# Graph layers on one Trainium2 core: the second message layer's attribute map computed with the first layer's, and smaller first pieces of the next layer's input

## The chip, the cores and the metric

The kernel runs on one core of a Trainium2 chip. The metric is the device time of one execution in microseconds (us); for the kernel before it is the median of three runs. A core has a matrix engine (TensorE, PE in the profile, with its weight loads as PEld), a vector engine (VectorE, DVE), an engine for functions of one element (ScalarE, ACT), GpSimd (POOL) and a queue engine (SyncE, SP). Matmuls read SBUF and write PSUM; DVE and ACT read both.

## The reference

A graph has N = 6250 nodes with 64 features and E = 200,000 edges, each with 16 attributes. First come two SAGE layers (mean over the incoming neighbours, a linear map, 64 to 128 to 64), a residual and a layer norm. Then come three message layers, which the change is about:

```python
def _mp_layer(x, src_f, dst_f, ea_f, W, b):
    m = concatenate([x[dst_f], x[src_f], ea_f], axis=1) @ W.T + b
    return relu(segment_sum(m, dst_f, num_segments=n))
h = _mp_layer(x, ..., W0, b0); h = relu(_batchnorm(h, g0, be0))
h = _mp_layer(h, ..., W1, b1); h = relu(_batchnorm(h, g1, be1))
h = _mp_layer(h, ..., W2, b2)
```

The edges include a self loop for each node with attributes of one. The result is a layer norm of x + h. Since the map is linear, a layer's sum over a node's edges falls into three parts: count times the node's own mapped features; the sum of the mapped features of its sources; and a part of the attributes alone, W's last 16 columns times the node's sum of attributes, and the bias times its count. The third part depends on no features, only on the layer's weights.

## The kernel before, in words

Nodes lie in NB = 49 blocks of P = 128; 4 blocks make a tile of TW = 512, of which there are NT = 13 (the last with one block). The kernel first builds the adjacency as dense fp8 counts, tile by tile (`build`), stores it in DRAM (`adj8`), and runs the first SAGE layer along with it. The second SAGE layer also builds the sums of attributes (`attributes`, L1008): `ext`, a tile of 128 partitions and 6272 nodes. Its rows 0 to 47 are the attribute sums three times (high, middle and low parts in bf16), rows 48 to 63 are zero, and rows 64 to 127 hold the node's count with the self loop. The weights for it are `extT[n]` (L577): three copies of the layer's attribute columns in rows 0 to 47 and the bias in row 64 = D (L603).

A sum over neighbours is `aggregate` (L640). For each block of destinations it adds 49 matmuls (`product`, L650): an adjacency block 128x128 as weights, and the source block's features as three bf16 parts side by side (192 columns) as the moving operand. With `terms`, one more float32 matmul per block, `term` (L657), adds the attribute part: 128 nodes of `ext` as weights and 64 columns of `extT[n]` moving, and it shows as two records. In layers two and three (n = 1, 2) `terms` is set (L1167). `add_parts` (L674) then adds the three parts on DVE.

Tiles 0 and 1 of a layer are done together and source by source (`src_first`), since their products can start as soon as the first sources are known; `feed` (L1171) makes the sources ready. In these two tiles the order before was: all eight terms, then for each source block `feed` and its eight products. `feed` calls `next_input` (L1108) for pieces of four blocks, one piece ahead: ACT makes `y` from the former layer's `hr` (a fused batch norm and ReLU, L1112), PE multiplies each block with `maps[n - 1]` into `u` (L1115), ACT and DVE split it into three bf16 parts (`split`, L626) and DVE makes the node's own part `own` (L1118, L1119). The matmuls of a program are reordered by a scheduler unless `pin` holds one behind the instruction that was written ahead of it on its engine.

At the end of a tile, layer one (`first_message`, L1125) transposes on PE (L700), copies on ACT (L702, `mx`), and multiplies with `catT[0]` (L1136) and `extT[0]` (L1137) into `lin`, of which ACT makes `hr` with a ReLU (L1138); layer two (`message_layer`, L1141) adds `own` (L1147), transposes into `tr` (L1151) and applies the ReLU on ACT (L1152). DVE takes the batch statistics of `hr` (L1123). Behind the last tile come `bn_aggr` (L1193), the square root on ACT (L1195) and four small DVE steps (L1196 to L1199) that give scale and shift `sc`. Only then can `next_input` of the following layer start. The adjacency tiles are loaded into three buffers, on SP's and ACT's queues in turn (`load_adj`, L677).

Of the kernel before, what the change touches and what calls it, by code (L numbers as in the profile page):

```python
# [11 lines left out]
F32 = mybir.dt.float32  # L12
# [462 lines left out]
def gnn_kernel(ctx: ExitStack, tc: tile.TileContext, x, src, dst, ea, W_l1, b_l1, W_r1, W_l2, b_l2, W_r2,  # L475
# [71 lines left out]
    with ExitStack() as fast:  # L547
# [22 lines left out]
        for n in range(3):  # L570


            if n == 0:
                catT.append(const.tile([2 * D, D], F32, name="catT"))
            else:
                maps.append(const.tile([D, 2 * D], F32, name=f"maps{n}"))
            extT.append(const.tile([P, D], F32, name=f"extT{n}"))  # L577
            nc.vector.memset(extT[n], 0.0)

        def load_weights():  # L580
            def transposed(to, of, at=0):
                p = psm.tile([P, P], F32, name="tr")
                k, m = of.shape
                pin(nc.tensor.transpose(p[:m, :k], of, ident[:k, :k]))
                nc.scalar.copy(to, p[:m, :k])

            def load(to, of):
                load.turn = not load.turn
                pin((nc.sync if load.turn else nc.scalar).dma_start(to, of))

            load.turn = False
            load(bl1, b_l1.rearrange("(p o) -> p o", o=1))
            load(bl2, b_l2.rearrange("(o d) -> o d", o=1).to_broadcast([P, D]))
            for to, w in ((w1s[:D, :], W_l1), (w1s[D:, :], W_r1), (w2s[:, :D], W_l2), (w2s[:, D:], W_r2)):
                t = spare(w.shape[1])[: w.shape[0], :]
                load(t, w)
                transposed(to, t)
            for n, (w, b) in enumerate(((W0, b0), (W1, b1), (W2, b2))):
                t = spare(2 * D + 3 * EC)[:D, :]
                for r in range(3):  # L600
                    load(t[:, 2 * D + r * EC: 2 * D + (r + 1) * EC], w[:, 2 * D:])
                load(t[:, : 2 * D], w[:, : 2 * D])
                load(extT[n][D: D + 1, :], b.rearrange("(o d) -> o d", o=1))  # L603
                if n == 0:
                    transposed(catT[0], t[:, : 2 * D])
                else:
                    transposed(maps[n - 1][:, D:], t[:, : D])
                    transposed(maps[n - 1][:, : D], t[:, D: 2 * D])
                transposed(extT[n][: 3 * EC, :], t[:, 2 * D:])
            for n, (g, be) in enumerate(((g0, be0), (g1, be1))):  # L610
                gam.append(const.tile([D, 1], F32, name=f"gam{n}"))
                bet.append(const.tile([D, 1], F32, name=f"bet{n}"))
                load(gam[n], g.rearrange("(p o) -> p o", o=1))
                load(bet[n], be.rearrange("(p o) -> p o", o=1))
# [25 lines left out]
        def aggregate(psa, pt, tiles, n, src_first=False, feed=None, terms=None, sources=range(NB)):  # L640

            views = [view(a, j) for a, j in tiles]
            sums = [psa.tile([P, 4, TW // 2], F32, name="agg") for _ in tiles]
            blocks = [(k, i) for k, (_, j) in enumerate(tiles) for i in range(tw(j) // P)]

            def product(k, i, b):

                nc.tensor.matmul(sums[k][:, i, :n], views[k][:, b, i * P: (i + 1) * P], pt[:, b, :n],  # L650
                                 start=(b == sources[0] and terms is None and not (src_first and i % 2)), stop=(b == sources[-1]),
                                 skip_group_check=src_first or terms is not None)

            def term(k, i):
                if terms is not None:
                    at = tiles[k][1] * TW + i * P
                    nc.tensor.matmul(sums[k][:, i, : terms[1].shape[1]], terms[0][:, at: at + P], terms[1],  # L657
                                     start=not (src_first and i % 2), stop=False, skip_group_check=True)

            if src_first:  # L660
                for k, i in blocks:
                    term(k, i)
                for b in sources:
                    feed(b)
                    for k, i in blocks:
                        product(k, i, b)
            else:
                for k, i in blocks:
                    term(k, i)
                    for b in range(NB):  # L670
                        product(k, i, b)
            return sums
# [61 lines left out]
        with ExitStack() as bld:  # L734
# [319 lines left out]
            hot = bld.enter_context(tc.tile_pool(name="ahot", bufs=2))  # L1054
            lhss = [ew.tile([P, EAG, P], BF16, name=f"lhs{k}", bufs=1) for k in range(2)]
            for lhs in lhss:
                nc.gpsimd.memset(lhs[:, :, 3 * EC: D], 0.0)
                nc.gpsimd.memset(lhs[:, :, D:], 1.0)
            selfl = ew.tile([P, 1], F32, name="selfl", bufs=1)
            nc.vector.memset(selfl, 0.0)  # L1060
            nc.vector.memset(selfl[:EC, :], 1.0)
            nc.vector.memset(selfl[D:, :], 1.0)


            per = -(-NSUB // NT)
# [33 lines left out]

        mp = fast.enter_context(tc.tile_pool(name="fmp", bufs=1))  # L1100
        hr = mp.tile([D, NPAD], F32, name="hr")
        own = mp.tile([P, NB, D], F32, name="own")
        ok_s = mp.tile([1, 1], I32, name="ok_s")
        psu = fast.enter_context(tc.tile_pool(name="fpsu", bufs=2, space=PSUM))
        nc.sync.dma_start(ok_s, ok_d)
        nc.vector.tensor_single_scalar(inv, cnt, 1.0, ALU.add)

        def next_input(n, b, sc, pt):  # L1108

            nb, s = min(4, NB - b), slice(b * P, min(b + 4, NB) * P)  # L1110
            y = work.tile([D, TW], F32, name="h1")
            nc.scalar.activation(y[:, : nb * P], hr[:, s], AF.Relu, bias=sc[:, 1:2], scale=sc[:, 0:1])  # L1112
            u = psu.tile([P, 4, P], F32, name="u")
            for i in range(nb):
                nc.tensor.matmul(u[:, i, :], y[:, i * P: (i + 1) * P], maps[n - 1], start=True, stop=True)  # L1115
            split(pt[:, b: b + nb, : 3 * D], u[:, :nb, :D], nb)
            o = own[:, b: b + nb, :]
            nc.vector.tensor_mul(o, u[:, :nb, D:], inv[:, b: b + nb].unsqueeze(2).to_broadcast([P, nb, D]))  # L1118
            nc.vector.tensor_add(o, o, u[:, :nb, :D])  # L1119
# [5 lines left out]
        def first_message(j, ps, stats):  # L1125

            w, s = tw(j), slice(j * TW, j * TW + tw(j))
            nb, bs = w // P, j * TW // P
            h = res[:, bs: bs + nb, :]
            nd = work.tile([P, 4, P], F32, name="nd")  # L1130
            nc.gpsimd.tensor_tensor(nd[:, :nb, :D], h, inv[:, bs: bs + nb].unsqueeze(2).to_broadcast([P, nb, D]), ALU.mult)  # L1131
            add_parts(nd[:, :nb, D:], ps, nb)
            nc.vector.tensor_add(nd[:, :nb, D:], nd[:, :nb, D:], h)
            both = transposed_tile(nd, nb)
            pm = psm.tile([P, TW], F32, name="lin")
            nc.tensor.matmul(pm[:D, :w], catT[0], both[:, :w], start=True, stop=False)  # L1136
            nc.tensor.matmul(pm[:D, :w], extT[0], ext[:, s], start=False, stop=True)  # L1137
            nc.scalar.activation(hr[:, s], pm[:D, :w], AF.Relu)  # L1138
            statistics(j, stats)

        def message_layer(n, j, ps, stats):  # L1141
# [6 lines left out]
            if n < 2:  # L1148
                t = psm.tile([P, 4, P], F32, name="tr")
                for i in range(nb):  # L1150
                    nc.tensor.transpose(t[:D, i, :], v[:, i, :], ident)  # L1151
                nc.scalar.activation(hr[:, s], t[:D, :nb, :].rearrange("f i p -> f (i p)"), AF.Relu)  # L1152
                statistics(j, stats)
                return
            nc.vector.scalar_tensor_tensor(v[:, :nb, :], v[:, :nb, :], 0.0, res[:, bs: bs + nb, :], ALU.max, ALU.add)
# [8 lines left out]
        sc = None  # L1164
        for n in range(3):
            pt = parts[n % 2]
            terms = (ext, extT[n]) if n else None  # L1167
            stats = work.tile([D, NT, nc.vector.BN_STATS_DIM], F32, name="stats") if n < 2 else None
            first = [(load_adj(j), j) for j in range(2)]

            def feed(b):  # L1171
                if n and b % 4 == 0:
                    if b == 0:
                        next_input(n, 0, sc, pt)
                    if b + 4 < NB:
                        next_input(n, b + 4, sc, pt)

            def message(j, ps):
                if n == 0:
# [11 lines left out]
                break  # L1191
            mv = work.tile([D, nc.vector.BN_AGGR_DIM], F32, name="mv")
            nc.vector.bn_aggr(mv, stats.rearrange("p j s -> p (j s)"))  # L1193
            sc = work.tile([D, 2], F32, name="sc")
            nc.scalar.activation(sc[:, 0:1], mv[:, 1:2], AF.Sqrt, bias=eps_t[:D])  # L1195
            nc.vector.reciprocal(sc[:, 0:1], sc[:, 0:1])  # L1196
            nc.vector.tensor_mul(sc[:, 0:1], sc[:, 0:1], gam[n])
            nc.vector.tensor_mul(sc[:, 1:2], mv[:, 0:1], sc[:, 0:1])
            nc.vector.tensor_sub(sc[:, 1:2], bet[n], sc[:, 1:2])  # L1199
        ok_r = nc.values_load(ok_s[0:1, 0:1], min_val=0, max_val=1)  # L1200

    with tc.If(ok_r == 0):
# [32 lines left out]
```

## Time and profile before

| | us |
|---|---|
| median of 3 runs (1628.0 to 1630.6) | 1628.94 |
| the profiled execution | 1625.03 |
| its span, first to last instruction | 1623.2 |
| PE busy in it | 1496.0 |
| DVE busy | 908.1 |
| ACT busy | 571.7 |
| products L650, 12,005 records | 1090.6 busy |

The span begins with the building of the adjacency; the three message layers start at about 919 us. The change from layer one to layer two lies at 1136 to 1151 us, the one from two to three at 1379 to 1390 us. Matmuls are pipelined, so the lengths of their records overlap, and the time that one takes is read from the starts. "Granted clock" is the share of its full clock that TensorE had in a stretch.

### The profile page before, as it was taken

Reading aid. Unit: us, or ns where it says so; the run is one execution under the profiler, and the core shown is the slowest. Engines: PE = TensorE matmul, PEld = TensorE weight load, DVE = VectorE, ACT = ScalarE, POOL = GpSimd, SP = SyncE. Lnnn points to the kernel's source line nnn. Section 1 sums busy time; section 2 is a strip of 40 time slices with the busy share of each in tenths; the row PEclk is TensorE's granted clock in tenths of the full one; section 3 lists DMA queues with packets and bytes.
Section 4 is the critical chain, followed back from the end, with each engine's and each line's share of the span. In section 5 each row is a group of like instructions: output and inputs, shape, how many; then the busy total and the mean of one; then the engine's idle time right before and its main releaser. Section 6 shows DMA issues by size and latency. Waiting matters only on the chain.

```text
span 1623.2 us, 38529 instructions
## 1 busy us (share of the span) xinstructions
PE 1496.0 (92%) x17135; PEld 1381.1 (85%) x17135; DVE 908.1 (56%) x1536; ACT 571.7 (35%) x1067; POOL 206.5 (13%) x94
## 2 busy tenths in 40 slices
PE   3687899999998999999999999999999999999997
PEld 1475787888887898999899988888899999899997
DVE  4999999997987618987986511111431111442222
ACT  2717475777866514444654200000310000310000
POOL 2344752441601100000000000000000000000000
PEclk9586899999999999999999999999899999899999
DMA  5121332140420645535344354443245443255440
GB/s 137 50 80 36 115 103 89 82 165 9 166 84 1 276 174 201 203 130 205 133 141 138 145 239 160 159 173 122 125 169 216 174 160 147 112 222 193 176 179 11
DMA packets 44432, 227.31 MB, mean 140 GB/s; under 512 B 23622, under 2 KB 30851, under 8 KB 36544
## 3 DMA queue, kind: packets, MB, share of 16 engines
q1 hardware_dynamic: 36571, 139.22, 22.8%
q10 hardware_dynamic: 4932, 78.28, 12.3%
q0 software_dynamic: 2752, 7.26, 1.5%
q8 instruction: 136, 2.23, 0.6%
q14 instruction: 41, 0.33, 0.1%
HBM read 183.77 MB, written 42.57 MB: 139 GB/s over the span
## 4 chain that ended last, share of the span: by engine, by line
PE 64%; DVE 19%; ACT 7%; issue 4%; DMA 4%; SPq 0%; ACTq 0%; POOL 0%; DVEq 0%
PE agg L650 48%; PE pair L962 7%; DVE lo L620 7%; ACT a L969 4%; DVE rhs L620 3%; PE u L1115 2%; PE bank L1029 2%; DVE e L1020 1%; DMA a<-adj 1%; DVE e L1022 1%; PE agg L657 1%; DMA e<-in_edge_attr_dram 1%; DVE nd L675 1%; DMA parts<-in_L_gnn_W_dram 1%; PE lin L1136 1%
## 5 line engine op out<-in xcount | busy, mean ns | idle before, releaser
L650 PE MATMUL agg<-parts,a 128*128 128x192 bf16 (+1 forms) x12005 | 1090.6, 246 | 3.1 <-DVE nd L675 1.7
L650 PEld LDWEIGHTS <-a 128*128 128x128 fp8e3 x12005 | 1007.4, 98 | 20.7 <-issue 11.8
L969 ACT ACTIVATE a<-pair 128x784 fp8e3<-128x784 f32 (+3 forms) x355 | 292.1, 894 | 113.8 <-PE pair L962 112.2
L962 PE MATMUL pair<-rhs,lo 128*128 128x147 bf16 (+5 forms) x2569 | 267.6, 245 | 53.1 <-DVE lo L620 19.0
L962 PEld LDWEIGHTS <-lo 128*128 128x128 bf16 x2569 | 198.8, 104 | 106.2 <-issue 49.0
L620 DVE TENSOR_TENSOR rhs<-iota,k 128x1960 bf16<-128x1960 f16 (+15 forms) x240 | 238.6, 1015 | 12.4 <-PE pair L962 10.4
L620 DVE TENSOR_TENSOR lo<-iota,k 128x2048 bf16<-128x2048 f16 x161 | 195.0, 1214 | 0.3 <-PE pair L962 0.3
L675 DVE TENSOR_REDUCE z<-agg 128x256 f32<-128x768 f32 (+1 forms) x39 | 35.3, 910 | 282.2 <-PE agg L650 281.9
L858 POOL DMA_INDIRECT rows<-ends,start_i x42 | 143.7, 3420 | 202.2 <-DVE key L870 157.1
L620 DVE TENSOR_TENSOR lo<-iota,e_d 128x2048 bf16<-128x2048 f16 (+11 forms) x132 | 130.8, 1011 | 20.5 <-PE bank L1029 18.3
L1029 PE MATMUL bank<-lo,lhs 128*128 128x128 bf16 x1701 | 107.5, 219 | 16.7 <-ACT lhs L1023 11.4
L1029 PEld LDWEIGHTS <-lhs 128*128 128x128 bf16 x1701 | 98.3, 98 | 28.2 <-ACT lhs L1023 19.5
L675 DVE TENSOR_REDUCE nd<-agg 128x256 f32<-128x768 f32 (+1 forms) x26 | 23.4, 905 | 116.0 <-PE agg L650 116.0
L1131 POOL TENSOR_TENSOR nd<-res,inv 128x256 f32<-128x256 f32 (+1 forms) x13 | 7.6, 588 | 549.1 <-DVE z L1078 339.2
L1123 DVE BATCH_NORM_STATS2 stats<-hr 64x6 f32<-64x512 f32 (+1 forms) x26 | 17.0, 652 | 101.7 <-ACT hr L1138 80.4
L702 ACT COPY mx<-tr 128x512 f32<-128x512 f32 (+1 forms) x26 | 14.7, 565 | 161.9 <-PE tr L700 161.9
L691 ACT ACTIVATE sp_r<-z 128x256 f32<-128x256 f32 (+1 forms) x26 | 10.5, 403 | 172.8 <-DVE z L690 172.8
L1152 ACT ACTIVATE hr<-tr 64x512 f32<-64x512 f32 (+1 forms) x13 | 7.3, 565 | 179.9 <-PE tr L1151 179.9
L1019 ACT CAST lhs<-e 128x512 bf16<-128x512 f32 (+21 forms) x72 | 36.1, 502 | 62.8 <-PE bank L1029 44.2
L821 POOL DMA_INDIRECT parts<-in_dst_dram,pos x22 | 41.7, 1897 | 50.8 <-DVE pos L816 38.3
L1020 DVE TENSOR_TENSOR e<-e,lhs 128x512 f32<-128x512 f32 (+21 forms) x72 | 39.4, 551 | 12.9 <-ACT lhs L1019 12.7
L1021 ACT CAST lhs<-e 128x512 bf16<-128x512 f32 (+21 forms) x72 | 36.3, 505 | 23.4 <-DVE e L1020 21.9
(131 smaller groups left out, 805.8 us busy)
## 6 DMA issues: line engine op xcount, KB each, us to landing
a<-adj SPq DMA_DIRECT2D x24, 3136.0 KB, 10.8
a<-adj ACTq DMA_DIRECT2D x24, 3136.0 KB, 11.5
adj<-a SPq DMA_DIRECT2D x12, 3136.0 KB, 10.7
e<-in_edge_attr_dram SPq DMA_DIRECT2D x25, 256.0 KB, 2.6
a<-adj SPq DMA_DIRECT2D x4, 784.0 KB
out_dram<-z SPq DMA_DIRECT2D x12, 128.0 KB, 6.4
e<-in_edge_attr_dram SPq DMA_DIRECT2D x7, 152.0 KB, 2.2
adj<-a SPq DMA_DIRECT2D x1, 784.0 KB
```

What stands on the lines that cost most here:

```text
L620: nc.vector.tensor_tensor(to.rearrange("p g (h two) -> p g h two", two=2), iota[:, :n].rearrange("p (h two) -> p h two", two=2).unsqueeze( ...
L650: nc.tensor.matmul(sums[k][:, i, :n], views[k][:, b, i * P: (i + 1) * P], pt[:, b, :n], start=(b == sources[0] and terms is None and not ( ...
L675: nc.vector.tensor_reduce(to, ps[:, :nb, : 3 * D].rearrange("p b (r d) -> p b d r", r=3), AX.X, ALU.add)
L821: pin(nc.gpsimd.indirect_dma_start(out=blks[t % most], out_offset=None, in_=dst.rearrange("(e o) -> e o", o=1), in_offset=bass.IndirectOff ...
L858: pin(nc.gpsimd.indirect_dma_start(out=rows[:, i, :], out_offset=None, in_=end[:, :], in_offset=bass.IndirectOffsetOnAxis(ap=start_i[:, t: ...
L962: nc.tensor.matmul(pair[:, bank % 2, col: col + wc], lo_hot(t, c), rhs[:, i, :wc], start=first, stop=last)
L969: nc.scalar.activation(av[:, :, o: o + 2 * nd].rearrange("p h (two d) -> p h two d", two=2), pair[:, :, : nd * NB].rearrange("p two (d h) ...
L1019: nc.scalar.copy(lhs[:, :g, 0:EC], r)
L1020: nc.vector.tensor_sub(r, r, lhs[:, :g, 0:EC])
L1021: nc.scalar.copy(lhs[:, :g, EC:2 * EC], r)
L1029: nc.tensor.matmul(ps[:, :P], lhs[:, q, :], oh[:, q % HOT, :], start=(c == 0 and q == 0), stop=(i == last_b[b] and q == g - 1))
L1115: nc.tensor.matmul(u[:, i, :], y[:, i * P: (i + 1) * P], maps[n - 1], start=True, stop=True)
```

## The change

The maps of layers one and two stand side by side in one tile `ext01` (128x128). In layer one the matmul with `ext` now gives 128 output rows: 64 for layer one and 64 for layer two's attribute part. DVE takes the latter out of PSUM, clamped to finite values, and puts it into rows 64 to 127 of `ext` (`e1`), which layer one has read by then. The bias moves to row 48, and the count's rows are 48 to 127, so the rows that stay (48 to 63) are enough. Layer two has no terms; instead DVE adds `e1` to the transposed sums ahead of the ReLU. Layer three keeps its terms, with `ext`'s 128 rows (the rows of `extT[2]` from 64 on are zero).

The order at the start of a layer changes: the first piece has one block, the second three, the others four; the matmuls `u` and the terms are pinned; the terms stand behind the first `feed`. In the scale's chain the mean is negated on its own and the last two DVE steps become one.

```diff
-            extT.append(const.tile([P, D], F32, name=f"extT{n}"))
+            if n == 0:
+                ext01 = const.tile([P, 2 * D], F32, name="ext01")
+            extT.append(ext01[:, n * D: (n + 1) * D] if n < 2 else const.tile([P, D], F32, name="extT2"))
...
-                load(extT[n][D: D + 1, :], b.rearrange("(o d) -> o d", o=1))
+                load(extT[n][3 * EC: 3 * EC + 1, :], b.rearrange("(o d) -> o d", o=1))
...
+                    if src_first:
+                        pin(first)
             if src_first:
-                for k, i in blocks:
-                    term(k, i)
                 for b in sources:
                     feed(b)
+                    if b == sources[0]:
+                        for k, i in blocks:
+                            term(k, i)
...
-                nc.gpsimd.memset(lhs[:, :, 3 * EC: D], 0.0)
-                nc.gpsimd.memset(lhs[:, :, D:], 1.0)
+                nc.gpsimd.memset(lhs[:, :, 3 * EC:], 1.0)
...
+        e1 = ext[D:, :]
...
-        def next_input(n, b, sc, pt):
+        def next_input(n, b, end, sc, pt):
...
-                nc.tensor.matmul(u[:, i, :], y[:, i * P: (i + 1) * P], maps[n - 1], start=True, stop=True)
+                pin(nc.tensor.matmul(u[:, i, :], y[:, i * P: (i + 1) * P], maps[n - 1], start=True, stop=True))
...
-            nc.tensor.matmul(pm[:D, :w], catT[0], both[:, :w], start=True, stop=False)
-            nc.tensor.matmul(pm[:D, :w], extT[0], ext[:, s], start=False, stop=True)
+            nc.tensor.matmul(pm[:, :w], ext01, ext[:, s], start=True, stop=False, skip_group_check=True)
+            nc.tensor.matmul(pm[:D, :w], catT[0], both[:, :w], start=False, stop=True, skip_group_check=True)
             nc.scalar.activation(hr[:, s], pm[:D, :w], AF.Relu)
+            nc.vector.tensor_scalar(e1[:, s], pm[D:, :w], 3e38, -3e38, ALU.min, ALU.max)
...
-                nc.scalar.activation(hr[:, s], t[:D, :nb, :].rearrange("f i p -> f (i p)"), AF.Relu)
+                nc.vector.tensor_add(hr[:, s], t[:D, :nb, :].rearrange("f i p -> f (i p)"), e1[:, s])
+                nc.scalar.activation(hr[:, s], hr[:, s], AF.Relu)
...
-            terms = (ext, extT[n]) if n else None
+            terms = (ext, extT[n]) if n == 2 else None
...
-                if n and b % 4 == 0:
-                    if b == 0:
-                        next_input(n, 0, sc, pt)
-                    if b + 4 < NB:
-                        next_input(n, b + 4, sc, pt)
+                ends = [1] + list(range(4, NB, 4)) + [NB]
+                if n and b == 0:
+                    next_input(n, 0, ends[0], sc, pt)
+                if n and b in [0] + ends[:-1]:
+                    q = ([0] + ends).index(b)
+                    if q + 1 < len(ends):
+                        next_input(n, ends[q], ends[q + 1], sc, pt)
...
+            nc.vector.tensor_single_scalar(mv[:, 0:1], mv[:, 0:1], -1.0, ALU.mult)
...
-            nc.vector.tensor_mul(sc[:, 1:2], mv[:, 0:1], sc[:, 0:1])
-            nc.vector.tensor_sub(sc[:, 1:2], bet[n], sc[:, 1:2])
+            nc.vector.scalar_tensor_tensor(sc[:, 1:2], sc[:, 0:1], mv[:, 0:1], bet[n], ALU.mult, ALU.add)
```

## The prediction

> **What bounds the kernel now.** I read the page first, then TensorE's timeline inside the message layers, then the chain of waits around the two layer changes, then the granted clock in stretches.
>
> ```profile
> span 1623.2 us, 38529 instructions
> PE 1496.0 (92%) x17135; PEld 1381.1 (85%) x17135; DVE 908.1 (56%) x1536; ACT 571.7 (35%) x1067; POOL 206.5 (13%) x94
> PEclk9586899999999999999999999999899999899999
> PE 64%; DVE 19%; ACT 7%; issue 4%; DMA 4%; SPq 0%; ACTq 0%; POOL 0%; DVEq 0%
> ```
>
> The change works behind 936 us, in the three message layers. TensorE (PE) carries the chain there: between 1195.0 and 1378.8 us it is busy 182.2 of 183.8 us, VectorE (DVE) 23.9, ScalarE (ACT) 7.1. What leaves PE in such a stretch leaves the time; what lands on DVE or ACT there is free. One block of the second layer (start, length, what):
>
> ```profile
> 1206.67 0.36 PE L657 MATMUL agg<-extT,ext 128*128 128x64 f32 x2
> 1206.87 4.21 PE L650 MATMUL agg<-parts,a 128*128 128x192 bf16 x49
> 1210.91 0.36 PE L657 MATMUL agg<-extT,ext 128*128 128x64 f32 x2
> ```
>
> The two records of a term (L657) start 0.20 us ahead of the products, and 49 products fill the other 4.04 us: lengths overlap, so I count starts. The chain at the change from layer one to two, and from two to three:
>
> ```profile
> 1136.67 1.76 PE agg L657 x16
> 1138.43 1.00 PE lin L1136 x2
> ...
> 1141.12 0.43 PE lin L1136 x2
> ...
> 1143.65 0.16 DVE sc L1198
> ...
> 1144.02 0.82 ACT h L1112
> 1144.84 0.04 issue
> 1144.89 3.79 PE u L1115 x16
> ```
> ```profile
> 1378.98 1.76 PE agg L657 x16
> 1380.74 0.12 PE tr L1151
> ```
>
> Both times eight terms of the next layer run ahead of the last matmuls of the old one, PE then idles 3.11 and 3.18 us while mean, variance and scale are formed and ACT makes a 512-column input (0.82 us). And the clock (stretch, busy PE and count, granted clock, DMA share, GB/s):
>
> ```profile
> 496.21:499.62 3.41, 1.41 (x11) 1.00 0.00 0
> 1141.33:1144.74 3.41, 0.44 (x4) 1.00 1.04 449
> 1144.74:1148.15 3.41, 3.26 (x15) 0.50 0.89 383
> 1148.15:1151.56 3.41, 3.32 (x17) 0.50 0.02 7
> 1151.56:1154.97 3.41, 3.41 (x23) 0.50 0.00 0
> 1154.98:1158.39 3.41, 3.41 (x41) 1.00 0.02 5
> ```
>
> In this trace the clock changes only on a grid of 3.41 us. A stretch with a thin PE is followed by half clock, and it comes back only behind a stretch full of products: the two full of 64-row `u` matmuls did not bring it back. At 1383.67 to 1393.91 it is the same: 10.2 us at half clock, some 5.1 us lost, at each layer change.
>
> **Terms of layer two, tiles 2 to 12.** 10 tiles of four blocks and one of one: 41 terms x 0.20 = 8.2 us off a full PE. Nothing is late in their place: a tile then takes 16.2 us, and the matrix loads land 10 to 13 us behind their issue with three buffers. In return each tile of layer one gets a DVE pass 64x512 out of PSUM (`e1`), and each of layer two an addition 64x512 ahead of the ReLU. Nearest row: 128x256 out of PSUM 0.42 us, so some 0.7 us each by columns. DVE has 160 us free there; inside the layers both cost nothing.
>
> **The wider attribute map, layer one.** Same two passes of 512 columns (0.59 us a record) with 128 output rows for 64; weight loads 0.19 for 0.14 us, beside running matmuls. The term now comes ahead of `catT`, which still waits for `mx`. 0, between -0.3 and +0.6 us over 13 tiles.
>
> **First layer change.** The eight terms go: `lin` of tile 11 starts at 1136.51 instead of 1138.36, 1.85 us, and the transpose of tile 12 behind it needs nothing later (its `nd` is ready at 1137.4). The scale chain loses one DVE step, 0.19 us (the negation runs under ACT's square root; if it holds that up, 0). The first input is one block: the nearest rows for 64x128 on ACT are 0.27 (the ReLU of tile 12) and 0.49 us (the last input); I take 0.3, near the ReLU, saving 0.5. `e1` of tile 12 (some 0.28 us) runs beside ACT's ReLU, which reads the other 64 partitions of the same bank. Here a rule speaks against the change: the Trainium skill, "PSUM — Partial Sum Buffer", section "PSUM bank collisions raise a hardware error", forbids two engines in one bank and one 32-partition quadrant at a time. The quadrants differ here, so no wait is owed; were one put in by bank, it would cost 0.3 to 0.9 us. No row of before shows it; I take 0. Sum: 2.55 us.
>
> **Second layer change.** Without terms ahead of it the transpose of tile 12 starts when its input is ready (1379.64) and not at 1380.58: 0.83. Scale chain 0.19, short input 0.5, less 0.3 for the added DVE step (128 columns 0.22 and a hop): 1.2 us gained. The terms are now pinned behind the first two `u` pieces: 16 records x 0.12 = 1.9 us of full-clock work that formerly lay partly in idle time. Behind them on PE are queued all products of the layer.
>
> **Pieces of one and three blocks, pinned.** `u` needs as many matmuls as before (98), but now one piece ahead instead of three. From the end of a `u` piece its split takes 2.3 us (1150.83 to 1153.11); behind it PE has 32 products and the next `u`, 2.75 + 1.08 = 3.8 us, so no stall. At the start `u` of blocks 1 to 3 covers the split of block 0 roughly: 0.1 us. The second adjacency tile, issued at 1131.73, lands at 1144.5, about when the first product would be ready: 0, up to 1 us.
>
> **The clock.** The rule: the Trainium skill, "TensorE: Matmul & The Clock Gate", Part 1, says half rate comes after an idle window of some 3.4 us and full rate after one busy window. By it the new gaps (3.11 - 0.7 = 2.4 us; 3.18 - 0.4 = 2.8 us) would keep full rate: another 5 us off at each change, sum 22. The trace decides otherwise: both old gaps are under 3.4 us and dropped, and at 496 us a stretch still 1.41 us busy dropped; return took three windows. I let both drop. When does the clock return? First change: the first long run of products is 24 x 0.165 = 4.0 us between `u` pieces, beginning 5.5 us in; a window fits it or the next run, 8 to 14 us in, against 10: 0, with 2 us either way. Second change: terms and the first products are 5.2 us of 128-row matmuls from 2.2 us on; a window fits by 4.6 to 8 us, mean 6.3 against 9.9: half of 3.6 us, 1.8 us gained. That counts the float32 terms as activity; if they don't, -2 instead. The second change: 1.2 - 1.9 + 1.8 = 1.1 us.
>
> **Rest.** Two memsets of ones instead of four on POOL, one more small one on DVE, a bias row at 48: 0, within 0.5.
>
> **Sum.** 8.2 + 2.55 + 1.1 = 11.9 us. The profiled execution took 1625.03 us (span 1623.2 and 1.8 around it) and would take 1613.1. The three timed runs have their median 3.9 us above it; I keep that: 1628.94 - 11.9 = 1617.0 us.
>
> **Rivals.**
> - As summed, 70%: 1613.5 to 1620.5 by the bounds above.
> - The clock survives a layer change, 12%: 5 us more for one (1612), 10 for both (1607). For: shorter gaps, and a grid line in mid-gap halves each side. Against: the drop at 496 us.
> - The layers start badly, 9%: `u` pieces between the first products keep a window from filling, so the half clock lasts one or two windows longer at each change (1.7 us each), or the second tile's load is awaited: 1620.5 to 1624.
> - The terms leave, but PE waits for something else (loads, sums' buffers), 4%: only the first layer change pays, 1626. Against: three buffers and 1.6 us of idle PE in 184 us.
> - Slower, 5%: the pinned order, one piece ahead. If split and own sums of a piece, sharing DVE and ACT with the next input, take longer than 3.8 us from `u`, every one of some 24 pieces stalls by the excess. It eats the 11.9 us from a split of 4.3 us on; at 5 us it costs 29 us, 1646. Against: 2.3 us in the trace.
>
> **How the numbers follow.** Likeliest 1617.0. Range 1609.5 to 1622.5: the first case, the clock surviving once, the milder half of the bad starts; about 15% is left out. About 0.2%, 3.3 us, is what a measurement can tell from no change. Faster 0.91, within 0.04 (lost gain), slower 0.05.
>
> **What would show it.** Records of L657 fall from 196 to 98, and the second layer's block from 4.24 to 4.04 us; if blocks stay at 4.24, the main step is wrong. PE's gaps at the layer changes shrink to about 2.4 and 2.8 us. Half clock is seen behind both, the second shorter than 10.2 us; a clock at 1.00 there is the second case. Idle PE ahead of products inside `u` pieces, released by the split's DVE step, would show the slower case.

## The result, and the profile after

The changed kernel takes 1623.66 us (median of 22 runs, 1619.84 to 1630.08), the kernel before beside it 1628.89 us (22 runs). The ratio is 0.9968, 95% interval 0.9958 to 0.9978: 5.2 us faster, where 11.9 us were forecast, and outside the stated range (1609.5 to 1622.5). The page of the changed kernel:

```profile
span 1624.3 us, 38372 instructions
PE 1489.5 (92%) x17037; PEld 1372.5 (84%) x17037; DVE 927.6 (57%) x1573; ACT 573.2 (35%) x1073; POOL 208.8 (13%) x92
PEclk9597899999999999999999999999899999899998
```

This span is 1.1 us longer than the one before, because the part ahead of the message layers took 926.8 us here and 919.1 us there. On all engines the instructions of that part stand in the same order in both kernels, save a few memsets (two of GpSimd became one, twice, and VectorE has one more). Over the eleven traces of this study it took 918.7 to 926.8 us with no link to the edits; two traces of the changed kernel itself have 926.8 and 920.8. So I cut what follows into stages, at starts that every trace has: A from the small checksum matmul (L1089 before) to the first `u` of layer two, B from there to the first `u` of layer three, C from there to PE's end. The stretches of before, and then of the changed kernel (length, busy PE, granted clock, DMA share, GB/s):

```profile
919.15:1144.89 225.74, 218.50 (x2324) 1.00 0.43 170
1144.89:1384.03 239.14, 234.31 (x2647) 0.98 0.40 160
1384.03:1612.54 228.51, 227.70 (x2581) 0.98 0.39 150
```
```profile
926.76:1149.69 222.93, 217.33 (x2307) 1.00 0.43 170
1149.69:1381.57 231.88, 224.05 (x2549) 0.98 0.42 166
1381.57:1613.37 231.80, 231.08 (x2597) 0.97 0.39 149
```

A gained 2.8 us and B 7.3 us, C lost 3.3 us: together 6.8 us, which the interval (3.6 to 6.8 us) just reaches. The records of terms are 98, as forecast. PE's timeline in layer two, first of the kernel before, from one tile's transposes to the next (17.64 us):

```profile
1216.91 0.60 PE L1151 MATMUL tr<-ident,z 128*64 128x128 f32 x4
1217.35 2.89 PE L650 MATMUL agg<-parts,a 128*128 128x192 bf16 x33
...
1232.98 1.48 PE L650 MATMUL agg<-parts,a 128*128 128x192 bf16 x16
1234.55 0.60 PE L1151 MATMUL tr<-ident,z 128*64 128x128 f32 x4
```

In the changed kernel a tile takes 16.97 us (1221.66 to 1238.63); the last four lines are the start of layer three with its terms:

```profile
1221.66 16.33 PE L652 MATMUL agg<-parts,a 128*128 128x192 bf16 x196
1238.20 0.60 PE L1159 MATMUL tr<-ident,z 128*64 128x128 f32 x4 [0.20 <-DVE z L1155]
1238.63 16.33 PE L652 MATMUL agg<-parts,a 128*128 128x192 bf16 x196
...
1377.97 0.27 PE L1159 MATMUL tr<-ident,z 128*64 128x128 f32 x1 [0.80 <-DVE z L1155]
1381.57 2.24 PE L1121 MATMUL u<-maps,h 64*128 64x128 f32 x8 [3.33 <-ACT h L1118]
1383.74 3.67 PE L659 MATMUL agg<-extT,ext 128*128 128x64 f32 x16
1387.20 1.49 PE L652 MATMUL agg<-parts,a 128*128 128x192 bf16 x8
```

The brackets give PE's idle time and what ended it: the transposes of every such tile now wait for VectorE, 0.20 us. The terms behind the first `u` pieces take 3.5 us from start to start, half speed. The matmul of layer one's last tile for which PE waits, before and then changed:

```profile
1141.12 0.43 PE L1136 MATMUL lin<-mx,catT 128*64 128x128 f32 x2 [0.57 <-ACT mx L702]
```
```profile
1145.87 0.49 PE L1142 MATMUL lin<-ext,ext 128*128 128x128 f32 x2 [1.15 <-DVE ext L1146]
```

The first layer change, in the chain of waits of the changed kernel (start, length):

```profile
1144.50 0.60 ACT hr L1144
...
1145.12 0.71 DVE ext L1146
...
1145.87 0.49 PE lin L1142 x2
...
1147.06 0.29 DVE ext L1146
...
1147.37 0.27 DVE stats L1129
...
1149.14 0.50 ACT h L1118
```

`e1` (L1146) does not run beside the ReLU (L1144): it starts when that has ended, here and in all 13 tiles of the layer. The last tile's matmul with `ext` waits for the first of these two `e1`, the last statistics for the second. And the clock at layer three's start:

```profile
1376.66:1380.07 3.41, 0.78 (x8) 1.00 1.08 461
1380.07:1383.48 3.41, 1.91 (x8) 0.50 0.98 419
1383.48:1386.89 3.41, 3.41 (x17) 0.50 0.97 419
1386.90:1390.31 3.41, 3.41 (x19) 0.50 0.53 228
1390.31:1393.72 3.41, 3.41 (x22) 0.50 0.00 0
```

Four stretches at half clock, not three. The third row is full from end to end, mostly with terms, and did not bring the clock back.

### The profile page after: what moved, and what is told of

The parts are those of the page before. It is cut to its first block, busy times and chain, and to the rows that moved or that the text cites. A ratio compares the mean times of both kernels' runs of the same rounds, so it can differ in the third digit from the quotient of the medians.

```text
span 1624.3 us, 38372 instructions
## 1 busy us (share of the span) xinstructions
PE 1489.5 (92%) x17037; PEld 1372.5 (84%) x17037; DVE 927.6 (57%) x1573; ACT 573.2 (35%) x1073; POOL 208.8 (13%) x92
## 4 chain that ended last, share of the span: by engine, by line
PE 65%; DVE 19%; ACT 7%; issue 4%; DMA 4%; SPq 0%; ACTq 0%; POOL 0%; DVEq 0%
PE agg L652 49%; DVE lo L622 7%; PE pair L967 7%; ACT a L974 4%; DVE rhs L622 3%; PE u L1121 2%; PE bank L1034 2%; DMA a<-adj 2%; DVE e L1025 1%; DVE z L680 1%; DVE e L1027 1%; DMA parts<-in_L_gnn_W_dram 1%; PE tr L705 1%; PE lin L1143 1%; PE lin L727 1%
## 5 line engine op out<-in xcount | busy, mean ns | idle before, releaser
L622 DVE TENSOR_TENSOR rhs<-iota,k 128x1960 bf16<-128x1960 f16 (+15 forms) x240 | 239.2, 1018 | 13.7 <-PE pair L967 11.8
L1161 ACT ACTIVATE hr<-hr 64x512 f32<-64x512 f32 (+1 forms) x13 | 7.9, 606 | 172.2 <-DVE hr L1160 172.2
L1146 DVE TENSOR_SCALAR ext<-lin 64x512 f32<-64x512 f32 (+1 forms) x13 | 8.6, 664 | 68.5 <-ACT hr L1144 68.5
```

Source lines behind the costliest of these rows:

```text
L622: nc.vector.tensor_tensor(to.rearrange("p g (h two) -> p g h two", two=2), iota[:, :n].rearrange("p (h two) -> p h two", two=2).unsqueeze( ...
```

## The experiments

Two theories stood against each other. Theory 1: the gain failed at layer three's start (terms at half clock, which also prolong it) and in the tiles of layer two. Theory 2: the small pieces pay, and layer two's interior loses to the added VectorE steps. Stages are from one trace of each run. The ratio, as recorded, is to the kernel before on the same chip; it is not the quotient of two medians of the table (for e1 that of its own chip would be 0.9936).

| run | A | B | C | sum | median | ratio (95%) |
|---|---|---|---|---|---|---|
| before | 225.7 | 239.1 | 228.5 | 693.4 | 1628.89 | |
| changed | 222.9 | 231.9 | 231.8 | 686.6 | 1623.66 | 0.9968 (0.9958 to 0.9978) |
| e0_after_again | 222.9 | 232.6 | 232.2 | 687.7 | 1621.45 | 0.9957 (0.9941 to 0.9974) |
| e1_map_only | 223.2 | 232.1 | 228.3 | 683.7 | 1617.59 | 0.9927 (0.9914 to 0.9941) |
| e2_terms_in_gap | 222.9 | 232.4 | 229.0 | 684.3 | 1619.33 | 0.9949 (0.9930 to 0.9967) |
| e4_pieces_only | 223.7 | 241.2 | 232.3 | 697.1 | 1630.49 | 1.0013 (1.0003 to 1.0023) |
| e3_bf16_for_terms | 222.9 | 233.5 | 231.2 | 687.6 | 1618.83 | 0.9945 (0.9929 to 0.9962) |
| e5_late_transposes | 219.6 | 228.5 | 228.2 | 676.3 | 1610.05 | 0.9900 (0.9883 to 0.9918) |
| e6_clock_kept | 222.9 | 228.7 | 227.3 | 678.9 | 1613.90 | 0.9919 (0.9902 to 0.9936) |
| e7_copy_on_scalar | 223.3 | 230.8 | 228.0 | 682.1 | 1616.11 | 0.9931 (0.9914 to 0.9947) |
| e8_both | 219.3 | 225.3 | 227.1 | 671.7 | 1604.64 | 0.9866 (0.9849 to 0.9882) |

**The control.** 

> The changed kernel as it stands, as a control on the same chip. I cut the time behind the build into three stages: A from the small checksum matmul to layer two's first input matmul, B from there to layer three's first input matmul, C from there to PE's end. The traces so far: before A 225.7, B 239.1, C 228.5 us; changed A 222.9, B 231.9, C 231.8. Both theories: the same stages within 0.5 us save where the half clock's grid falls otherwise (1.7 us a step), and a time some 0.3% under the kernel before. The part ahead of A has the same instruction streams in both kernels and differed by 7.6 us between the two traces; both theories expect it to scatter.

Nearly as expected: A and C repeat within 0.4 us, B within 0.7 (0.5 was expected). A difference of that size between two traces is no finding.

**The two halves of the change.** The map alone:

```diff
-                ends = [1] + list(range(4, NB, 4)) + [NB]
+                ends = list(range(4, NB, 4)) + [NB]
...
-                pin(nc.tensor.matmul(u[:, i, :], ...))
+                nc.tensor.matmul(u[:, i, :], ...)
...
+                for k, i in blocks:
+                    term(k, i)
                 for b in sources:
                     feed(b)
-                    if b == sources[0]: ...
```

The pin on the terms goes too.

> The attribute map as changed; pieces of four blocks, no pins, and layer three's terms ahead of the first input, as before the change. Theory 1 (the missing gain was lost at the start of layer three, where the pinned terms run at half clock behind the first input matmuls and do not bring the clock back): A 223.4, B 233, C back to 228.5, so 1 to 2 us less than the changed kernel. Theory 2 (the gain was lost inside layer two, to the added DVE steps, and the small first pieces pay what they were summed at): B as changed or worse, C still near 231.8 or higher for want of small pieces, so 1 to 3 us more than the changed kernel.

C fell to 228.3 as theory 1 had it, and B did not rise. The kernel is faster than the changed one: 3 us by the stages; by the ratios of this run and of the control, measured on the same chip, 0.9927 and 0.9957, whose intervals just touch.

The other half, on the kernel before: small pieces and pins, and its terms, in layers two and three, behind the first `feed`:

> The kernel before with the pieces of one and three blocks, the pins, and the terms of layers two and three behind the first input piece; its attribute maps and its scale chain are those of before. Theory 1: A 223.5 (terms gone from ahead of the last matmuls), B about 241 and C 231.8, each with 3.3 us of terms at half clock: some 2 to 3 us slower than the kernel before. Theory 2 (small pieces pay): faster than before by 1 to 3 us.

Slower than before, as theory 1 had it: 0.13%, some 2 us, in the timed runs and 3.7 us by the stages. A gained 2.0 us, about the 1.85 us of the terms that no longer stand ahead of layer one's last matmuls, and B and C lost 5.9. Both layers' half clock lasted 13.7 us in its trace. Theory 2 falls: the first half of the change is worth more than the whole, the second costs. This run moves the terms together with the pieces; the next one has the pieces without the terms behind them.

**The terms in the gap.** As changed, with the loop of terms written ahead of the loop over sources, pinned:

> As changed, but layer three's eight terms are written and pinned ahead of the first input piece, so that PE runs them in the idle gap behind the last transpose. Theory 1: C falls by the 3.7 us that the terms took at half clock, to about 228, B stays at 231.9 (1.9 us of terms fit the 3.3 us gap), and with the gap down to 1.4 us the half clock may not come at all, which would take a further 5 us off C. Theory 2 (what fails at layer three's start is the interleaving of small pieces, not the terms): C falls by 1.9 us at most and the half clock still lasts 13.7 us.

C fell by 2.8 us, between the two theories. The 3.5 us of the terms left, and other waits came to light: the first products waited 0.28 us for the split and those of the second tile 0.35 us for its adjacency load. The half clock lasted 10.2 us. In the timed runs the gain is not clear: 0.9949 against the control's 0.9957, with intervals that overlap. Against e1, which has its terms ahead of the first input too, the small pieces bring nothing: 684.3 us for 683.7. That the half clock came at all is the surprise. PE's idle time was down to 1.59 us, split by a line of the grid:

```profile
1377.37:1380.78 3.41, 2.05 (x18) 1.00 0.95 402
1380.78:1384.19 3.41, 2.24 (x8) 0.51 1.04 449
```

Of the 2.05 busy us, 1.9 are terms. So I asked whether float32 terms count as activity. The row alone doesn't say so: in the trace of before a stretch with 1.94 us of bf16 matmuls (287.99 to 291.40) was followed by half clock as well.

**Products in the terms' place.** 24 bf16 products into an unread bank; the terms go behind the products of later sources:

```diff
                     if b == sources[0]:
-                        for k, i in blocks:
-                            term(k, i)
+                        busy(24)
                     for k, i in blocks:
                         product(k, i, b)
+                    if 0 < b <= len(blocks):
+                        term(*blocks[b - 1])
```

> As changed, but at layer three's start 24 bf16 products into a PSUM bank that nobody reads stand where the eight float32 terms stood (about as long at half clock, 4.0 us), and the terms come one by one behind the products of sources 1 to 8. The output is the same. Theory 1a (float32 terms of 64 columns hardly count as activity, so they held the clock down for a further window): the half clock at layer three's start lasts 6.8 to 10.2 us instead of 13.7, and C is 230.4 to 232.1 us though 2.0 us of work were added. Theory 1b (terms count like products, and it is the input matmuls between the groups that keep the clock down): still 13.7 us, C 233.8.

The half clock at layer three lasted 6.8 us, and C was 231.2, in spite of the added work:

```profile
1376.80:1380.21 3.41, 0.30 (x2) 1.00 1.03 441
1380.21:1383.62 3.41, 3.37 (x18) 0.50 0.99 427
1383.62:1387.03 3.41, 3.41 (x24) 0.50 0.97 419
1387.03:1390.44 3.41, 3.41 (x37) 1.00 0.04 15
```

The third row has the place of the one full of terms in the changed kernel; here it brought the clock back. At layer two's start, where nothing was edited, this run had 13.7 us for the changed kernel's 10.2: how the grid falls moves one step of 3.4 us (1.7 us of time) from run to run. Two steps less, as here, against 13.7 in both traces of the changed kernel, is more than that, but it is one trace.

The other traces agree. At four starts of a layer terms stood behind the first `u` pieces (layer three in both traces of the changed kernel, both layers in e4), and all four had 13.7 us. Of the 13 other half clocks at a layer's start, without the bf16 products of this run, eleven lasted 10.2 us, one 13.7 (this run's layer two) and one 6.8 (layer two in e7). Counted from start to start, a stretch at half clock at these changes was followed by full clock if it held 1.90 us of products or more (changed kernel, 1154.79), and by half clock if it held 1.85 or less (this run, 1151.50), whatever terms or `u` filled of the rest.

It is not the type alone. While the adjacency is built, wider float32 matmuls did lift the clock. The kernel before, two stretches and PE's timeline in the first:

```profile
281.17:284.58 3.41, 3.25 (x9) 0.50 0.08 19
284.58:287.99 3.41, 1.94 (x22) 1.00 0.07 19
```
```profile
281.14 2.07 PE L722 MATMUL lin<-mx,w1s 128*128 128x512 f32 x2 [0.56 <-ACT mx L702]
283.01 0.83 PE L962 MATMUL pair<-rhs,lo 128*128 128x147 bf16 x5
283.99 0.98 PE L727 MATMUL tr<-w2s,h 128*128 128x128 f32 x4 [0.16 <-ACT h L724]
```

Some 2.4 us of this stretch are float32 matmuls with 128 rows and 512 or 128 columns moving, and only some 0.8 us are bf16. Nine more of the eleven traces have such a stretch; three others, with 2.2 to 2.35 us of the float32, did not bring it back.

**The transposes.** In layers one and two a tile's sums and transposes are written behind the first block of the next tile:

```diff
                     for b in range(NB):
                         product(k, i, b)
+                    if i == 0 and between is not None:
+                        between()
```

> The map-only kernel, with a tile's sums, transposes and what follows written behind the first block (49 products) of the next tile in layers one and two, so that PE does not meet the transposes before VectorE has their input. Theory 1 (part of the 0.20 us per term was not gained because the term had covered a wait for VectorE ahead of the transposes, 0.2 to 0.4 us in each tile): layer two's tile falls from 16.97 to about 16.65 us and layer one's from 19.2 to about 18.95, B by 3 us to 229, A by 2 us to 221. Theory 3 (the tile's rest is another cost, of the products or of PE's own): tiles stay within 0.05 us of 16.97 and 19.2.

The tile of layer two is 16.6 us, that of layer one 18.8. From the transposes on, 196 products now take 16.17 us from start to start, and PE does not wait ahead of the next transposes any more:

```profile
1213.58 16.33 PE L652 MATMUL agg<-parts,a 128*128 128x192 bf16 x196
1229.75 0.60 PE L1158 MATMUL tr<-ident,z 128*64 128x128 f32 x4
1230.18 1.98 PE L652 MATMUL agg<-parts,a 128*128 128x192 bf16 x22
```

A and B gained 3.6 and 3.7 us over the map alone; I had expected 2 and 3. The kernel before had part of this wait too, though no bracket shows it in layer two: of its 17.20 us from the first product behind one tile's transposes to the next transposes (1217.35 to 1234.55), products take 16.17 and the four terms 0.80, so 0.23 us were lost there, against 0.37 in the changed kernel.

**The clock.** As changed, with 32 and 36 unread products in the gaps, 12 behind the first `u` pieces, and the terms behind later sources:

```diff
+                busy(idle[2] if idle else 0)
                 for b in sources:
                     feed(b)
```

> As changed, with bf16 products that nobody reads in PE's idle time: 32 behind layer one's last matmul, 36 behind layer two's last transpose, and 12 behind the input matmuls of the first four blocks; layer three's terms come one by one behind the products of sources 1 to 8. The output is the same. Theory 1a (the clock follows the share of bf16 products in a stretch of 3.41 us): no half clock at either change or a shorter one, B from 231.9 to 227, C from 231.8 to 226. Theory 1b (input matmuls or the whole change of layer drop it anyway): half clock as before at both, B and C unchanged or up to 1 us longer.

No half clock at either change. The stretches around the first:

```profile
1136.61:1140.02 3.41, 2.52 (x19) 1.00 1.00 424
1140.02:1143.43 3.41, 3.15 (x33) 1.00 1.01 434
1143.44:1146.85 3.41, 3.07 (x30) 1.00 0.99 427
1146.85:1150.26 3.41, 3.41 (x38) 1.00 0.55 233
```

B fell by 3.2 us, C by 4.5, less than the 4.9 and 5.8 expected. I take it that the unread products behind `u` are themselves on the path (12 take 1.0 us at full clock); no run leaves them out.

**The bank.** The map alone, with `e1` taken by `nc.scalar.copy` in place of `nc.vector.tensor_scalar`:

> The map-only kernel, with layer two's part taken out of PSUM on ScalarE behind the ReLU instead of on VectorE (the clamp is left out: this input has no infinities). Theory 1 (at the first layer change VectorE's pass waited for ScalarE's ReLU because both read one PSUM bank, and the last tile's statistics stood behind it, 0.3 us): A falls by 0.3 us from 223.2, statistics of the last tile start right behind the ReLU. Rival (the wait was VectorE's own): A unchanged. ScalarE's longer queue could take it all back: the last tile's matmul waits for the copy too, up to 0.6 us more.

PE's gap at the first change fell from 3.29 to 2.98 us, the 0.3 us of the statistics. A as a whole stayed (223.3 for 223.2): in this trace PE waited 0.46 us for `nd` ahead of one tile's transposes (at 980.22), which the map alone did not, and I don't know whether that is the copy's doing. B's 230.8 is a half clock of 6.8 us, a step of the grid. The run shows that the statistics had stood behind `e1`; it doesn't settle why `e1` waited for the ReLU, by bank or otherwise. A bank of its own for it was not tried.

**Both.** 

> The late transposes of layers one and two together with the products that nobody reads in the gaps (and the changed kernel's small pieces, layer three's terms behind the products of sources 1 to 8). The output is the same. If the two causes are separate, as theory 1 has it, their gains add: A 219.6, B 231.9 - 3.7 - 3.2 = 225.0, C 227.3, together 672 us against 693.4 before and 686.6 as changed, a ratio to the kernel before of about 0.987. If one of them only uncovers the other's wait (the loads of the second adjacency tile, VectorE's queue), A + B + C stays above 675.

The gains add: 671.7 us, 1604.64 us in the timed runs, 1.3% under the kernel before and the fastest version here.

## Why the prediction was wrong

The direction, the main step and PE as the bound were right: a block's products do take 4.04 us in the changed kernel (16.17 for four). The sum was 5.1 us too high by the traces (11.9 against 6.8): 3.2 us of it at layer three's start, where the terms kept the half clock up, and 1.3 us in the tiles of layer two, where a wait took the terms' place. The time falls into the rival "the layers start badly" (9%), and its mechanism, a half clock one window longer, came at one of the two changes; the loss in the tiles is not part of it. By steps:

- **Terms of layer two, tiles 2 to 12: 8.2 forecast, some 6.9 measured** (17.64 less 16.97 is 0.67 us a tile, over 10 tiles and a quarter). The sentence "Nothing is late in their place" failed; its tile of 16.2 us was four blocks without their transposes. A term was 0.20 us of work, but one per tile stood between a tile's end and its transposes, which wait for VectorE's sums; without it the loss there rose from 0.23 to 0.37 us. e5 shows the wait: with the transposes put behind a block of products a tile takes 16.6 us.
- **First layer change and layer one: 2.55 forecast, 2.8 measured,** near by luck, since errors cancel. `e1` was costed at nothing beside the ReLU, from the Trainium skill's "PSUM — Partial Sum Buffer" (bank collisions), by which different quadrants owe no wait. The trace has a wait: 0.94 us of idle VectorE, released by ACT's `hr`, 0.6 of them while the ReLU ran. It held the last matmul 0.6 us (PE's idle time there rose from 0.57 to 1.15) and the statistics 0.3. The short input also took 0.50 us and not 0.3. Against that, layer one's tiles became shorter, from 19.3 to 19.2 us, about 1 us in all; I had 0 for it. The matmul of `ext` now stands ahead of the transposes, and their wait for `nd`, 0.25 us before, is gone from the timeline; no run tests that this is the reason.
- **Second layer change, ahead of `u`: 1.2 forecast, about 0.7 measured** (from tile 11's transposes to `u`, 8.37 us before and 7.64 after): the short input again (0.50 us for 0.3), and tile 11's statistics, which now stand between the last tile's addition and its own statistics and end 0.3 us later than those alone would have.
- **Second layer change, the clock: the step that failed most.** "That counts the float32 terms as activity" was the choice between +1.8 and -2 us, and I chose wrong. The clock was to return 4.6 to 8 us behind the first `u`; it returned after 12.2 (1381.57 to 1393.72). The stretch full of terms did not lift it, and the half clock lasted 13.7 us instead of 10.2, which costs 1.7 us on top of the terms' 1.9 us of work. C lost 3.3 us where the sum had 0.1. e1 and e2 got most of it back by moving the terms ahead of `u`. In e3, with bf16 products in their place, the half clock was two windows shorter, but the added work ate nearly all of that (C 231.2 for 231.8).
- **The clock at both changes: right that it would drop.** The Trainium skill's "TensorE: Matmul & The Clock Gate" (Part 1) has half rate after an idle window of about 3.4 us and full rate after one busy window. Here the clock dropped behind gaps of 2.97 and 3.33 us, even behind one of 1.59 (e2), and its return took two to four windows. The same page's advice to leave no idle gaps above about 3 us (section "Why this matters for your kernels") was too mild here, with drops at 2.97 and 1.59; with bf16 products in the gaps and 0.23 and 0.36 us of idle time left ahead of `u`, the clock stayed (e6). The gaps themselves did not shrink to 2.4 and 2.8 us: the short input took 0.50 us and the statistics ended later.
- **Pieces of one and three, pinned:** no stall in the steady state, as forecast (each piece 3.83 us, as before), so the slower case did not come. But they bring next to nothing: at the first change the changed kernel is 0.3 us ahead of e1 in A and level in B, and with the terms ahead of the input in both, e2 is 0.7 us behind e1 in C, the size of the scatter.

What stays open: what makes the terms count for so little, since wide float32 matmuls did lift the clock (their 64 columns were not varied), and what makes `e1` wait for the ReLU.

## What to carry to other kernels

Work that is taken off a full engine is gained only where nothing else stands at its place: look what the removed instruction lay in front of, and whether that waits for another engine. In a gap between phases put the moved work into the idle time, not behind it, where it runs at the clock that the gap has left. Count a gap's activity in the matmuls that the clock was seen to follow.

## What the runs showed of the hardware

A stretch of 3.41 us full of float32 matmuls, most of them terms (128 rows, 64 columns moving), did not lift the half clock (changed kernel, 1383.48); one full of bf16 products did (e3, 1383.62), and so did one with 2.4 us of float32 matmuls of 512 and 128 columns (before, 281.17). 32 bf16 products in 2.8 us of otherwise idle PE, with 12 more behind the first `u` pieces, kept the full clock across a change of layer; B was 3.2 us shorter (e6). The part ahead of the message layers, the same on all engines but for a few memsets, took 918.7 to 926.8 us in eleven executions, and 926.8 and 920.8 in two of one kernel.
